# Moving small waits of TensorE in a two-layer transformer block: scale transposes behind products, a bias behind the next normalisation, expert transposes in another PSUM ring, ranks inside a gate pair

## The chip, the cores and the metric

The kernel runs on one core of one Trainium2 chip. The metric is the device time of one launch in microseconds (us); lower is better. All times below are microseconds unless marked ns.

## The reference

`x` is 8 x 256 rows of 512 numbers (2048 rows in all), `ctx` is a context of the same shape. Four residual steps follow each other:

```python
x = x + L0_xattn(ctx, ctx, layernorm(x), ssm_kernel, D, 8)   # long convolution of k*v pairs along 512, times q
x = x + L0_ffn(layernorm(x), w1, b1, w2, b2)                  # two "bit" linears, 512 -> 2048 -> 512
x = x + L1_xattn(layernorm(x), ctx, ...)                      # 16 heads of 32, 256 queries x 256 image keys per batch
x = x + L1_ffn(layernorm(x), ...)                             # 2 shared experts + top 2 of 16 routed experts

def _bitlinear(x, w, b):
    xq = round(layernorm(x) * 127 / max|.|) ...               # per row, 8 bits
    wq = clip(round(w / mean|w|), -1, 1) * mean|w|            # ternary weights
    return einsum('bsd,fd->bsf', xq, wq) + b
# L0_ffn: bitlinear(gelu(bitlinear(x, w1, b1)), w2, b2)
# L1_xattn: softmax(rms_norm(x@Wq+bq)*gq . rms_norm(ctx@Wk_img+bk)*gk / sqrt(32)) @ v, then @ Wo + bo
# L1_ffn: x + shared + sum over the two best experts of p_e * expert_e(x),
#         expert(x) = (gelu(x@g + gb) * (x@w1 + b1)) @ w2 + b2
```

## The kernel before

The 2048 rows live in SBUF as 16 tiles of 128 x 512 (`xs`). Five stages follow each other, and inside each stage the order of instructions on every engine is the order of the Python code (`in_order`); a scheduler does not move them. Each engine works its own queue strictly in turn, so an instruction that waits holds everything behind it on its engine.

**Stage 1, long convolution** (to about 185 us): a loop over 32 heads (`head`, called with `between`, which slips in small pieces of the next stage: `second_norm`, `mixed`, and `ahead`, the generators `Pair.gradually` that normalise and quantise the first two pairs of row tiles piece by piece).

**Stage 2, the bit FFN** (about 185 to 380): a software pipeline over eight pairs of tiles, `f0` to `f7` (class `Pair`). For a pair, `split` (GpSimd/POOL) cuts a per-row scale `u` into three bf16 parts; `turn_x` transposes the quantised rows on TensorE (PE) into `xT`, which ScalarE (ACT) copies to `xq`; `turn_u` transposes the scale parts into `uT`, which ACT copies to `ub` (L384). `hidden(i, half)` makes 8 products `xq` by `w1q` (L399), 2 bias products `ub` by `b1k` (L404), and a GELU on ACT (L408). `mean`, `centre` (L422), `squares` (L430, ACT), `largest` (L435, DVE), `scales`, `scales_back`, `rounded_back` (L453, VectorE/DVE) quantise the hidden rows; `turn_back` transposes them (`hT`, PE) and ACT copies them to `hq`; `back` makes 16 products (L473). In step `g` of the loop, pair `g` is in `hidden`, pair `g-1` is being quantised, pair `g-2` is in `turn_back` and `back(0)`, pair `g-3` in `back(1)`, and pair `g+1` is being normalised. PSUM rings: `tr` (two buffers) for all transposes, `conv` (two) for the hidden products, `mm` (two) for `op`.

**Stage 3, attention** (about 380 to 749): 64 steps; a step holds four heads' half, steps go in twos. In loop turn `n`: `normalise` of step n-1 (POOL, `pr`, L1244), exponentials of an odd step (ACT, L1235), scores of two steps (PE, `sc`), `turn` of step n-2 (8 transposes `pt`, L1255, ring `tr`), pieces of the next batch (`middle`, `value`, `end`: `k_mm`, `q_mm`, `v_mm`, their transposes), `values` (`o`, ring `mm`), and each fourth turn `project_out` (`fo`, ring `mm`), whose result DVE adds to `xs` (L1287) and to which POOL adds the output bias `bo` (L1288). In the last turns (`at` = n-56) there is no further batch; ACT normalises finished tiles for the experts (`dxn`, L1374), and `turn_in` transposes them (`dxT`, ring `tr`) and DVE copies them to `xT` (L1314).

**Stage 4, shared experts on half the rows and routing** (about 749 to 847): `gate` makes 4 fp32 products for one gate or up projection (`gu`, L1504), `gated` the GELU and product. The generator `route` (`pieces`) is drawn out between them: it computes on DVE which experts each row takes (`both`, L1573), counts ranks by 17 small products on PE (`rank`, L1577 on), derives the slots on DVE, and scatters the rows to DRAM by 32 indirect DMAs from POOL (L1633).

**Stage 5, routed experts** (about 847 to 1061): `Unit` (256 rows) and `Double` (2 x 64 rows). A unit loads weights and its gathered rows `xr` (SP queue), `turn` transposes them (`r_xTp`, L162, ring `gh`) and ACT copies them to `r_xT` (L1676), `products` (L1689) and `back` (L1705) follow. Then the shared experts on the other half of the rows, gathering, and the store.

Of the kernel before, what the change touches and what calls it, by code (L numbers as in the profile page):

```python
# [11 lines left out]
AF = mybir.ActivationFunctionType  # L12
ALU = mybir.AluOpType
# [6 lines left out]
DC = D // P  # L20
NT = B * S
H, HD = 32, 8
# [3 lines left out]
FF = 2048  # L26
# [52 lines left out]
def tile_kernel(ctx: ExitStack, tc: tile.TileContext, a: dict, out: bass.AP):  # L79
    nc = tc.nc  # L80
# [17 lines left out]
    zero = column(0.0, "zero")  # L98
# [59 lines left out]
    def transposed(pool, src, name, tag, chunks=range(DC)):  # L158

        ps = pool.tile([P, DC, P], F32, tag=tag, name=name)  # L160
        for at, c in enumerate(chunks):
            nc.tensor.transpose(ps[:, at, :], src[:, c * P : (c + 1) * P], ident)  # L162
# [123 lines left out]
    class Pair:  # L286
# [32 lines left out]
        def gradually(self):  # L319

            nm = self.nm
            self.mv = stat.tile([P, 2, 2], F32, tag="mv", name=nm + "_mv")
            for i in range(2):
                moment(self.mv[:, i, :], self.T[i], f"{nm}{i}")
                yield
            nmean = stat.tile([P, 2], F32, tag="nmr", bufs=2, name=nm + "_nm")
            times(nmean, self.mv[:, :, 0], -1.0)
            self.factor()
            yield
            self.xc = fp.tile([P, 2, D], F32, tag="xc", bufs=2, name=nm + "_xc")  # L330
            for i in range(2):
                nc.scalar.activation(
                    self.xc[:, i, :], self.T[i], AF.Identity, bias=nmean[:, i : i + 1]
                )
            yield
            self.largest_x()
            yield
            qs = self.scales_x()
            for i in range(2):
                nc.scalar.activation(  # L340
                    self.xc[:, i, :], self.xc[:, i, :], AF.Identity, bias=qmagic,
                    scale=qs[:, i : i + 1],
                )
            yield
            self.split()

        def largest_x(self):
            self.amax = stat.tile([P, 2], F32, tag="amax", name=self.nm + "_amax")
# [43 lines left out]
        def hidden(self, i, half):  # L392

            hp = pp.tile([P, FF // 2], F32, tag="conv", name=f"{self.nm}_hp{i}{half}")
            for q in range(2):
                cols = bass.ts(2 * half + q, D)
                dst = hp[:, q * D : (q + 1) * D]
                for c in range(DC):
                    nc.tensor.matmul(  # L399
                        dst, lhsT=self.xq[:, i, c, :], rhs=w1q[:, c, cols], start=(c == 0), stop=False  # L400
                    )
            for q in range(2):
                cols = bass.ts(2 * half + q, D)
                nc.tensor.matmul(  # L404
                    hp[:, q * D : (q + 1) * D], lhsT=self.ub[:, i, :], rhs=b1k[:, cols],
                    start=False, stop=True,
                )
            nc.scalar.activation(  # L408
                self.hs[i][:, bass.ts(half, FF // 2)], hp, AF.Gelu, bias=zero,
                scale=self.s1[:, i : i + 1], accum_out=self.hsum[:, i, half : half + 1],  # L410
            )

# [43 lines left out]
            self.hq = [None, None]  # L456

        def turn_back(self, i, half):
            if half == 0:
                self.hq[i] = fp.tile([P, FC, P], BF16, tag="hq", bufs=2, name=f"{self.nm}_hq{i}")  # L460
            ps = turned_halves(
                pp, [self.hs[i][:, bass.ts(2 * half + k, D)] for k in range(2)], f"{self.nm}_hT{i}{half}"
            )
            nc.scalar.activation(
                self.hq[i][:, bass.ts(half, 2 * DC), :], ps.rearrange("p i c q -> p (i c) q"),
                AF.Identity, bias=nhalf,
            )

# [283 lines left out]
    def between():  # L752
        if unfinished:
            sums(*unfinished)
        if 1 <= h <= 13:
            next(norm1)
        elif 17 <= h <= 24:
            next(mixed0)
        elif h > 24:
            next(ahead[0], None)  # L760
        for _ in range((0, 1, 3)[max(h - H + 3, 0)]):
            next(ahead[1])

    for g in range(H // G):
        kv, qx = following
        for hh in range(G):
            h = g * G + hh
# [227 lines left out]
    def more_mixed():  # L995
        for _ in range(2):
            next(mixed1)

    one, two, three = pairs[:3]
    one.turn_x()  # L1000
    one.turn_u()
    one.hidden(0, 0)
    for _ in ahead[1]:
        pass
    more_mixed()
    one.hidden(0, 1)
    more_mixed()
    one.hidden(1, 0)
    more_mixed()
    one.hidden(1, 1)  # L1010
    more_mixed()

    mix.__exit__(None, None, None)
# [4 lines left out]
    wsb = {}  # L1018
# [34 lines left out]
    one.largest(1)  # L1053
    one.squares(1)
    one.scales()
    two.hidden(1, 1)
    one.scales_back()
    three.turn_x()
    two.mean()
    one.rounded_back()  # L1060
    for g in range(2, 8 + 2):
# [66 lines left out]
            continue  # L1128
        if left:
            left.back(1)  # L1130
        if p:
            p.turn_u()
        if mid:
            mid.centre()
            mid.largest(0)
        if left:
            left.update(1)
            left.add_bias()
        if mid:
            mid.squares(1)  # L1140
        if p:
            p.hidden(0, 0)
        last.turn_back(0, 0)
        if coming:
            coming.moments()
        if mid:
            mid.largest(1)
        prepare(0)
        if p:
            p.hidden(0, 1)  # L1150
        last.turn_back(0, 1)
        if coming:
# [40 lines left out]
    with tc.tile_pool(name="att", bufs=2) as ap_, tc.tile_pool(  # L1193
# [10 lines left out]
        class Step:  # L1204
# [60 lines left out]
            def values(self, before):  # L1265
# [11 lines left out]
                            )  # L1277
                nc.scalar.copy(self.oT[:, 2 * cp : 2 * cp + 2, :], op)

        def project_out(b, i, oT):  # L1280
# [7 lines left out]
            nc.gpsimd.tensor_tensor(T, T, wsb["bo"], ALU.add)  # L1288

        class Norm:  # L1290

# [18 lines left out]
        done_norms = {}  # L1310

        def turn_in(t, xn):
            ps = transposed(pc, xn, f"dxT{t}", "tr")
            nc.vector.tensor_copy(xTs[t // 4][:, :, t % 4 * P : (t % 4 + 1) * P], ps)  # L1314


# [9 lines left out]
        for n in range(len(steps) + 4):  # L1326
# [9 lines left out]
                    coming = batches[steps[n].b + 1]  # L1336
            if 0 < n <= len(steps):
                steps[n - 1].normalise()
            if coming:
                coming.begin(k)  # L1340
            if n < len(steps) and n % 2:
# [14 lines left out]
                    coming.value(k - 4)  # L1356
                coming.end(k)
            at = n - (len(steps) - 8)
            if at in (-3, -1):
                batches[-1].value((at + 3) // 2)  # L1360
            if at == 1:

                nmr = stat.tile([P, 8], F32, tag="nmr8", bufs=1, name="d_nmr")
# [28 lines left out]
                    project_out(s.b, s.i, s.oT)  # L1392
            if n in later:
                project_out(later[n].b, later[n].i, later[n].oT)

            for t in NORMED.get(at - 1, ()):
                turn_in(t, done_norms[t])
# [423 lines left out]
    order = [lambda e=e: Unit(f"r{e}", e, NS * P * e, NS * P) for e in range(E)]  # L1821
    for j in range(NO1 // 2):
        order.insert(4 * j + 3, lambda j=j: Double(j))
    units = [order[0]()]
    units[0].turn()
    for i in range(len(order)):
        if i + 1 < len(order):
            units.append(order[i + 1]())
        units[i].products()
        if i:  # L1830
            units[i - 1].turn_back()
        if i + 1 < len(order):
# [126 lines left out]
```

## Time and profile before

Three runs took 1156.17 us in the median (1151.67 to 1158.35).

| what | us |
|---|---|
| time of the profiled execution | 1151.6 |
| its span, first to last instruction | 1149.8 |
| PE busy | 1094.3 (95%) |
| DVE / ACT / POOL busy | 683.6 / 520.8 / 440.2 |
| mean granted TensorE clock | 0.999 |
| chain that ended last | PE 76%, DVE 14%, POOL 4% |

A row of a timeline has the start, the length, the engine and line, the operation, what it writes and reads, how many were merged, and in brackets how long its engine had idled before it and which instruction's end let it go. "PE pt L1255 <- DVE xT L1314" in the table of waits reads: PE stood before its instruction on `pt` until DVE's instruction on `xT` had ended. Busy PE is modelled from pipelined matmuls; the idle time between them is what this document argues with.

### The profile page before, as it was taken

How to read it: one execution, taken by the hardware profiler on the slowest of the kernel's cores; microseconds unless marked ns; L12 is line 12 of the kernel's file. 1: busy time of each engine (PE TensorE's matmuls, PEld its weight loads, DVE VectorE, ACT ScalarE, POOL GpSimd, SP SyncE). 2: the span in 40 equal slices, each digit the busy share in tenths (PEclk: the TensorE clock that was granted, in tenths of full speed). 3: DMA queues.
4: the chain of work that ended last, by engine and by line, in shares of the span. 5: the costliest groups of instructions: out<-in, count | busy, mean ns of one | idle time of the engine just before them, and what ended most of it. 6: DMA issues, size and time to landing. Idle time of an engine off the chain costs nothing.

```text
span 1149.8 us, 16488 instructions
## 1 busy us (share of the span) xinstructions
PE 1094.3 (95%) x5866; PEld 658.8 (57%) x5885; DVE 683.6 (59%) x1507; ACT 520.8 (45%) x1173; POOL 440.2 (38%) x501
## 2 busy tenths in 40 slices
PE   4999998899999999999999998899999999999997
PEld 3777775454545555555655555554466766675443
DVE  5998999798866565765656756637612222222452
ACT  4437645798884555656556565531011121111000
POOL 5788887244331243433333434313770000000650
PEclk9999999999999999999999999999999999999999
DMA  7424520699500100000000010052668999997571
GB/s 272 154 74 150 153 76 20 236 305 291 141 1 19 37 1 4 16 19 1 20 20 1 2 38 1 1 194 102 240 202 269 306 338 330 301 314 240 155 248 40
DMA packets 122780, 153.26 MB, mean 133 GB/s; under 512 B 7481, under 2 KB 81273, under 8 KB 122178
## 3 DMA queue, kind: packets, MB, share of 16 engines
q1 hardware_dynamic: 108608, 116.49, 32.1%
q10 hardware_dynamic: 8962, 18.85, 4.6%
q0 software_dynamic: 5120, 16.78, 4.4%
q8 instruction: 49, 0.80, 0.3%
q14 instruction: 41, 0.34, 0.1%
HBM read 107.66 MB, written 44.43 MB: 132 GB/s over the span
## 4 chain that ended last, share of the span: by engine, by line
PE 76%; DVE 14%; POOL 4%; issue 2%; ACT 1%; DMA 1%; SPq 1%; POOLq 0%; DVEq 0%; ACTq 0%
PE r_h L1689 10%; PE gu L1504 9%; PE y L693 5%; PE k_mm L865 5%; PE fo L1284 5%; PE v_mm L865 5%; PE r_po L1705 5%; PE q_mm L865 5%; PE po L1526 5%; PE pt L1255 5%; PE f_op L473 2%; PE sc L1219 2%; PE f_hp L399 2%; PE o L1274 2%; PE o_h L1746 2%
## 5 line engine op out<-in xcount | busy, mean ns | idle before, releaser
L1244 POOL TENSOR_TENSOR pr<-pr,rden 128x1024 f32<-128x1024 f32 x64 | 121.1, 1893 | 155.8 <-DVE rden L1242 140.6
L693 PE MATMUL y<-kv,tp 128*128 128x288 f32 x640 | 161.7, 408 | 5.2 <-DVE wl L716 5.0
L693 PEld LDWEIGHTS y<-kv,tp 128*128 128x128 f32 x640 | 119.0, 190 | 42.5 <-PE y L693 10.1
L1235 ACT ACTIVATE pr<-sc,mx 128x256 f32<-128x256 f32 x256 | 118.3, 483 | 8.1 <-DVE mx L1227 6.9
L1842 POOL DMA_INDIRECT yg<-yd,slot x32 | 33.1, 1035 | 224.4 <-PE gu L1504 206.3
L1689 PE MATMUL r_h<-r_xT,r_gu 128*128 128x256 f32 x512 | 113.7, 380 | 1.5 <-ACT r_xT L1676 1.5
L1689 PEld LDWEIGHTS r_h<-r_xT,r_gu 128*128 128x128 f32 x512 | 96.8, 190 | 22.4 <-issue 8.0
L1227 DVE TENSOR_REDUCE mx<-sc 128x4 f32<-128x1024 f32 x64 | 77.5, 1212 | 4.5 <-PE sc L1219 4.5
L1255 PE MATMUL pt<-ident,pr 128*128 128x128 f32 x512 | 70.6, 279 | 7.5 <-DVE xT L1314 3.5
L1696 DVE SCALAR_TENSOR_TENSOR r_y<-r_h,eb,r_ge 128x256 f32<-128x256 f32 x32 | 15.5, 483 | 97.7 <-PE r_h L1689 94.4
L1260 ACT COPY pts<-pt 128x512 f32<-128x512 f32 x64 | 37.8, 590 | 73.2 <-PE pt L1255 73.2
L1255 PEld LDWEIGHTS pt<-ident,pr 128*128 128x128 f32 x512 | 55.0, 140 | 26.1 <-issue 14.6
L1695 ACT ACTIVATE r_ge<-r_h,gb 128x256 f32<-128x256 f32 x32 | 15.1, 473 | 109.0 <-PE r_h L1689 109.0
L399 PE MATMUL f_hp<-w1q,f_xq 128*128 128x512 bf16 x245 | 59.4, 379 | 5.3 <-ACT f_xq L376 4.5
L631 POOL TENSOR_TENSOR kv<-kx 128x2048 f32<-128x2048 f32 x16 | 57.6, 3601 | 12.9 <-ACT kx L617 12.9
L865 PE MATMUL k_mm<-Wk_sb,cx 128*128 128x512 f32 x128 | 58.1, 598 | 0.0
L865 PE MATMUL v_mm<-Wv_sb,cx 128*128 128x512 f32 x128 | 57.7, 593 | 0.0
L1705 PE MATMUL r_po<-r_w,r_y 128*128 128x512 f32 x128 | 57.7, 593 | 0.0
L1284 PE MATMUL fo<-Wo_sb,oT 128*128 128x512 f32 x128 | 57.7, 593 | 0.0
L865 PE MATMUL q_mm<-Wq_sb,xT 128*128 128x512 f32 x128 | 57.6, 593 | 0.0
L1516 ACT ACTIVATE ge<-gu,gb 128x512 f32<-128x512 f32 x16 | 11.0, 687 | 102.6 <-PE gu L1504 93.8
L473 PE MATMUL f_op<-w2q,f_hq 128*128 128x512 bf16 x249 | 57.0, 379 | 0.4
(486 smaller groups left out, 2104.5 us busy)
## 6 DMA issues: line engine op xcount, KB each, us to landing
xd<-blank SPq DMA_DIRECT2D x1, 15360.0 KB, 59.2
tp<-kpd SPq DMA_DIRECT2D x32, 256.0 KB, 3.3
r_gu<-in_rg SPq DMA_DIRECT2D x16, 512.0 KB, 6.6
r_gu<-in_rw SPq DMA_DIRECT2D x16, 512.0 KB, 6.8
r_w<-in_rw SPq DMA_DIRECT2D x16, 512.0 KB, 6.8
r_xr<-xd SPq DMA_DIRECT2D x16, 512.0 KB, 6.9
yd<-r_yo ACTq DMA_DIRECT2D x32, 256.0 KB, 5.7
yd<-blank SPq DMA_DIRECT2D x1, 6144.0 KB, 77.9
```

What stands on the lines that cost most here:

```text
L399: nc.tensor.matmul(dst, lhsT=self.xq[:, i, c, :], rhs=w1q[:, c, cols], start=(c == 0), stop=False)
L473: nc.tensor.matmul(op, lhsT=self.hq[i][:, c, :], rhs=w2q[:, c, :], start=(c == 0), stop=(c == FC - 1))
L693: nc.tensor.matmul(y[:, ll, :, 0:PAIRS], lhsT=tp[:, dl : dl + P], rhs=view(kv, (m0 * G + hh) * PAIRS, [[G * PAIRS, B], [1, PAIRS]]), start ...
L865: nc.tensor.matmul(t, lhsT=lT[:, c, i * P : (i + 1) * P], rhs=w[:, c, :], start=(c == 0), stop=(c == DC - 1),)
L1227: nc.vector.tensor_reduce(self.mx, self.sc.rearrange("p r c k -> p (r c) k"), AX.X, ALU.max, negate=True)
L1235: nc.scalar.activation(self.pr[:, h // 2, h % 2, :], self.sc[:, h // 2, h % 2, :], AF.Exp, bias=self.mx[:, h : h + 1], accum_out=self.den[ ...
L1244: nc.gpsimd.tensor_tensor(flat, flat, rden.unsqueeze(2).to_broadcast([P, 4, S]), ALU.mult)
L1255: nc.tensor.transpose(pt[:, cc, k, :], self.pr[:, rr, cc, k * P : (k + 1) * P], ident)
L1284: nc.tensor.matmul(fo, lhsT=oT[:, c, :], rhs=wsb["Wo"][:, c, :], start=(c == 0), stop=(c == DC - 1))
L1504: nc.tensor.matmul(ps, lhsT=w[0][:, c, k, f * P : (f + 1) * P], rhs=xTs[tb][:, c, :], start=(c == 0), stop=(c == DC - 1),)
L1689: nc.tensor.matmul(ps, lhsT=self.w[0][:, c, k, f * P : (f + 1) * P], rhs=self.xT[:, c, 0:n], start=(c == 0), stop=(c == DC - 1),)
L1705: nc.tensor.matmul(po, lhsT=self.y[:, f, i * P : (i + 1) * P], rhs=self.w[1][:, f, :], start=(f == 0), stop=(f == EC - 1),)
```

## The change

Every instruction stays; only places in the queues and one PSUM ring change.

1. *FFN start.* `split` moves ahead of the last `yield` of `gradually`, so that it is drawn one head earlier. Of the second pair's pieces one less is drawn in the last head; that piece (ACT, centring of `f1_xc`) comes after `turn_u` of the first pair. The first pair's first two `hidden` follow each other; the four pairs of `mix` transposes come later, the last four tiles in a row.
2. *FFN, pair f2.* `turn_u` comes before the loop, and ACT makes `xq` and `ub` of f2 ahead of f1's last GELU. In step 2 both halves of `hidden(0)` come ahead of the first `hT`.
3. *FFN, steps 3 to 7.* The two `uT` transposes, and the eight transposes of the first `hT`, move from either side of the first `hidden` to between its 8 products and its 2 bias products. ACT's order stays: `ub`, `squares`, GELU, `hq`.
4. *Attention.* POOL's bias add goes behind the `normalise` of the following turn. `turn_in` takes ring `mm` in place of `tr`. The last batch's first `value` moves from turn 53 to 52.
5. *Routing.* The rank products go between the gate and the up projection of one pair, not ahead of both; the DVE, ACT and POOL orders do not change by it.
6. *Routed experts.* The second unit's transposes move ahead of the first unit's products. On SP only one load of `o0_xr` changes places with one of `r3_gu`.

```diff
@@ Pair.gradually
+            self.split()
             yield
-            self.split()
@@ Pair.hidden is now product + gelu
+        def hidden(self, i, half, between=None):
+            self.product(i, half, between)
+            self.gelu(i, half)
 ...                                    # 8 products
+            if between:
+                between()
 ...                                    # 2 bias products
@@ Pair.turn_back is now turn (PE) + turned (ACT)
@@ between, in the heads
-        for _ in range((0, 1, 3)[max(h - H + 3, 0)]):
+        for _ in range((0, 1, 2)[max(h - H + 3, 0)]):
@@ FFN start
     one.turn_u()
+    next(ahead[1])
     one.hidden(0, 0)
+    one.hidden(0, 1)
+    more_mixed()
     for _ in ahead[1]:
         pass
-    more_mixed()
-    one.hidden(0, 1)
-    more_mixed()
     one.hidden(1, 0)
     more_mixed()
     one.hidden(1, 1)
+    more_mixed()
     more_mixed()
@@
-    two.hidden(1, 1)
+    two.product(1, 1)
     one.scales_back()
     three.turn_x()
+    three.turn_u()
+    two.gelu(1, 1)
     two.mean()
@@ loop over g
-        if p:
-            p.turn_u()
 ...
-        if mid:
+        def turns():
+            if g > 2:
+                p.turn_u()
             mid.squares(1)
+            if g > 2:
+                last.turn(0, 0)
         if p:
-            p.hidden(0, 0)
-        last.turn_back(0, 0)
+            p.hidden(0, 0, turns)
+        if g == 2:
+            p.hidden(0, 1)
+        if g == 2 or not p:
+            last.turn(0, 0)
+        last.turned(0, 0)
@@ attention
-            nc.gpsimd.tensor_tensor(T, T, wsb["bo"], ALU.add)
+            biased.append(T)          # added by add_output_bias(), called behind normalise()
-            ps = transposed(pc, xn, f"dxT{t}", "tr")
+            ps = transposed(pc, xn, f"dxT{t}", "mm")
-            if at in (-3, -1):
-                batches[-1].value((at + 3) // 2)
+            if at in (-4, -1):
+                batches[-1].value((at + 4) // 3)
@@ shared experts and routing
-    for (tb, e, f), n in zip(rest, (2, 3, 3, 3, 3, 2)):
-        gated(tb, e, f, gate_up(tb, e, f, shw[e]), yTs[tb])
+    for (tb, e, f), n in zip(rest, (0, 2, 3, 3, 3, 3)):
+        first_gate = gate(tb, e, f, shw[e], 0)
         for _ in range(n):
             next(pieces)
+        gated(tb, e, f, (first_gate, gate(tb, e, f, shw[e], 1)), yTs[tb])
+    for _ in range(2):
+        next(pieces)
@@ routed experts
-    units = [order[0]()]
-    units[0].turn()
+    units = []
+    for i in range(2):
+        units.append(order[i]())
+        units[i].turn()
     for i in range(len(order)):
-        if i + 1 < len(order):
+        if 0 < i < len(order) - 1:
             units.append(order[i + 1]())
```

More of the change, by code (lines that the diff above doesn't have):

```diff
@@ L390, in turn_u, with product @@
             self.hsum = stat.tile([P, 2, 2], F32, tag="hsum", name=nm + "_hsum")
-        def hidden(self, i, half):
+        def hidden(self, i, half, between=None):
+            self.product(i, half, between)
+            self.gelu(i, half)
+        def product(self, i, half, between=None):
             hp = pp.tile([P, FF // 2], F32, tag="conv", name=f"{self.nm}_hp{i}{half}")
+            self.hp = hp
             for q in range(2):
@@ L407, in hidden, with gelu @@
                 )
+        def gelu(self, i, half):
             nc.scalar.activation(
-                self.hs[i][:, bass.ts(half, FF // 2)], hp, AF.Gelu, bias=zero,
+                self.hs[i][:, bass.ts(half, FF // 2)], self.hp, AF.Gelu, bias=zero,
                 scale=self.s1[:, i : i + 1], accum_out=self.hsum[:, i, half : half + 1],
@@ L458, in turn_back, with turn, turned @@
         def turn_back(self, i, half):
+            self.turn(i, half)
+            self.turned(i, half)
+        def turn(self, i, half):
             if half == 0:
                 self.hq[i] = fp.tile([P, FC, P], BF16, tag="hq", bufs=2, name=f"{self.nm}_hq{i}")
-            ps = turned_halves(
+            self.ps = turned_halves(
                 pp, [self.hs[i][:, bass.ts(2 * half + k, D)] for k in range(2)], f"{self.nm}_hT{i}{half}"
             )
+        def turned(self, i, half):
             nc.scalar.activation(
-                self.hq[i][:, bass.ts(half, 2 * DC), :], ps.rearrange("p i c q -> p (i c) q"),
+                self.hq[i][:, bass.ts(half, 2 * DC), :], self.ps.rearrange("p i c q -> p (i c) q"),
                 AF.Identity, bias=nhalf,
@@ L1148, in tile_kernel @@
         prepare(0)
-        if p:
+        if p and g > 2:
             p.hidden(0, 1)
@@ L1278, in values @@
                 nc.scalar.copy(self.oT[:, 2 * cp : 2 * cp + 2, :], op)
+        biased = []
         def project_out(b, i, oT):
@@ L1287, in project_out, with add_output_bias @@
             nc.vector.tensor_tensor(T, T, fo, ALU.add)
-            nc.gpsimd.tensor_tensor(T, T, wsb["bo"], ALU.add)
+            biased.append(T)
+        def add_output_bias():
+            while biased:
+                T = biased.pop()
+                nc.gpsimd.tensor_tensor(T, T, wsb["bo"], ALU.add)
         class Norm:
@@ L1338, in tile_kernel @@
                 steps[n - 1].normalise()
+            add_output_bias()
             if coming:
@@ L1394, in tile_kernel @@
                 project_out(later[n].b, later[n].i, later[n].oT)
+            if n == len(steps) + 3:
+                add_output_bias()
             for t in NORMED.get(at - 1, ()):
@@ L1831, in tile_kernel @@
             units[i - 1].turn_back()
-        if i + 1 < len(order):
+        if 0 < i < len(order) - 1:
             units[i + 1].turn()
```

## The prediction, made before the changed kernel ran

> **What bounds the kernel now.** I read the busy times first, then the chain that ended last, then PE's waits by releaser, then windows by stage, and last the timeline around each wait.
>
> ```profile
> PE 1094.3 (95%) x5866; PEld 658.8 (57%) x5885; DVE 683.6 (59%) x1507; ACT 520.8 (45%) x1173; POOL 440.2 (38%) x501
> PE 76%; DVE 14%; POOL 4%; issue 2%; ACT 1%; DMA 1%; SPq 1%; POOLq 0%; DVEq 0%; ACTq 0%
> ```
>
> TensorE is busy for 1094.3 of 1149.8 us, so all its idle time is 55.5 us. No instruction is removed; the change can only win parts of those 55.5 us, where PE waits for something that is late. PE's waits by releaser (total, count, mean) show which of them it aims at:
>
> ```profile
> PE f_uT L382 <- POOL u L366: 4.5, 4, 1.4
> PE f_hp L399 <- ACT f_xq L376: 4.5, 3, 2.2
> PE pt L1255 <- DVE xT L1314: 3.5, 5, 1.9
> PE pt L1255 <- POOL pr L1244: 3.2, 3, 2.0
> PE rank L1577 <- DVE both L1573: 1.8, 1, 1.8
> PE f_hp L404 <- ACT f_ub L384: 1.8, 1, 1.8
> PE r_h L1689 <- ACT r_xT L1676: 1.5, 2, 0.7
> PE qT_tr L162 <- DVE pts L1262: 1.3, 1, 1.3
> ```
>
> These are 22.1 us in all: the most that could be won here if every one vanished and none came back. The windows say where another engine would take over (length, then busy PE, PEld, DVE, ACT, POOL, the clock, DMA share, GB/s):
>
> ```profile
> 245.00:338.00 93.00, 89.95 (x559) 47.41 (x571) 77.23 (x141) 80.84 (x94) 39.73 (x89) 1.00 0.63 176
> 682.00:749.00 67.00, 57.68 (x553) 36.18 (x552) 42.19 (x83) 38.77 (x130) 29.49 (x18) 1.00 0.01 1
> ```
>
> In the FFN's steady part ACT (87%) and DVE (83%) stand close behind PE (97%), so a wait won there can come back. In the attention's tail nothing but PE is above 63%: there, waits are matters of order, and can be moved.
>
> **FFN start (edit 1): 2.1 us.** Before, `uT` waited 1.35 for `split`, which POOL did at 193.20 to 194.97, and the first product waited 1.55 for `xq`, which stood on ACT behind `f1_xc` (194.63, 1.33 long). Drawn one head earlier, `split`'s nine instructions (1.8 us) find `f_u` ready at 188.16 and POOL idle from 187.05 to 190.82: they hide there; without that cover they would delay the next head's combination by up to 1.8. `uT` follows `xT` at once, `xq` runs at 193.73 to 194.83, and the first product starts at 194.85 instead of 197.02: 2.17 earlier. The four `mix` groups now come last, where two buffers and DVE's adds (0.64 each) make PE wait about 0.85 in place of 0.38 + 0.34. `f1_xc`, moved behind `xq` and `ub`, ends at 196.5; its own transposes come about 208, and cover it. Bounds: 1.5 to 2.5. I take 2.1.
>
> **Pair f2 and steps 3 to 7 (edits 2 and 3): 2.9 us.** These rows of before carry it:
>
> ```profile
> 224.35 1.90 PE L399 MATMUL f_hp<-w1q,f_xq 128*128 128x512 bf16 x8 [2.18 <-ACT f_xq L376]
> 225.75 2.00 ACT L418 ACTIVATE f_h<-f_h,f_hm 128x2048 f32<-128x2048 f32 x1 [1.45 <-DVE f_hm L115]
> 242.59 2.47 DVE L453 TENSOR_SCALAR f_h<-f_h,f1hq_qs 128x2048 f32<-128x2048 f32 x2
> 242.72 1.19 POOL L365 CAST f_up<-f_u 128x2 bf16<-128x2 f32 x1
> 245.17 0.44 PE L382 MATMUL f_uT<-ident,u 128*128 128x128 f32 x2 [0.88 <-POOL u L366]
> ```
>
> At 224.35 PE waited 2.18 for `xq`, which stood behind a GELU (1.20); now it stands ahead, so about 1.0 goes. The 1.81 for `ub`, queued behind `mean` (225.75, which itself waits for DVE's `f_hm`), goes whole, since `ub` comes ahead too. But that does not shorten `mean`: the GELU of f2's first half still follows `mean` (to 227.65), `squares` (2.00) and itself (1.19), to 230.95, and the third `hidden` needs its `conv` buffer. So PE, now early, waits about 2.35 there, and starts it at 230.95 where it started at 231.56: of 2.8 won, 0.6 is left, and the two `hT` wait for no one. In steps 3 to 7, `uT` waited 0.88, 1.18 and 1.12 (3.18 in all) for `u`; between the products it comes 1.73 after them (L399 to L404: 245.44 to 247.17), with the 16 products before it ending at 244.29 at about 245.9, and `u` is ready at 245.11. What is late next is `ub`, 2.20 after the first product, and behind it on ACT `squares` (2.00) and the GELU (1.19): with 0.27 for `ub` the buffer is free at 5.66 after it, and PE wants it at 5.47 (16 products 3.46, 4 of bias 0.86, `uT` 0.27, two groups of `hT` 0.88): 0.15 to 0.2 a step, 0.75 in five. The stretch's waits were (with f1's `xq`, 0.77, and one for a GELU, 0.24) 0.77 + 0.24 + 2.18 + 1.81 + 3.18 = 8.2, and becomes 0.77 + 0.24 + 1.18 + 2.35 + 0.75 = 5.3. Bounds: zero, if ACT and DVE take the loop whole, to 5.4, if the 2.35 and 0.15 don't appear.
>
> [...]
>
> **Attention's tail (edit 4): 4.7 us.**
>
> ```profile
> 708.80 1.26 POOL L1288 TENSOR_TENSOR xs<-xs,bo_sb 128x512 f32<-128x512 f32 x1 [3.82 <-DVE rden L1242]
> 710.03 3.75 POOL L1244 TENSOR_TENSOR pr<-pr,rden 128x1024 f32<-128x1024 f32 x2
> 711.98 1.09 PE L1255 MATMUL pt<-ident,pr 128*128 128x128 f32 x8 [2.03 <-POOL pr L1244]
> 731.48 0.39 ACT L1278 COPY oT<-o 128x256 f32<-128x256 f32 x1
> 732.82 0.66 PE L1255 MATMUL pt<-ident,pr 128*128 128x128 f32 x4 [1.89 <-DVE xT L1314]
> ```
>
> At 708.80 the bias takes POOL for 1.26 ahead of `pr` that PE waits 2.03 for; `rden` was there at 708.81. Behind it, `pr` starts 1.23 earlier: 1.23. The bias then runs 1.89 later; it is read by the moments of finished tiles, which come much later, and by `dxn`. Around 686 to 692 three waits (0.87, 1.28, 0.17) would be covered by `v_mm`, moved there (8 products, 3.44), but `oT`'s copy then stands on ACT for `o`, the exponentials behind it end at 691.2, and the scores come at about 692.3 instead of 693.6: 1.3. With `dxT` in ring `mm`, the transposes `pt` no longer need DVE's copy of `xT` to free a `tr` buffer: waits of 0.35, 0.35, 1.89, 0.51 and 0.44 go. At the 1.89 the next `fo` finds `oT` only at 731.87, so 1.4 of it counts; and in `mm` new small waits come, for `oT` or `xT`'s copy ahead of `fo` (0.3 at 722, 0.4 at the end): 2.2 net. Sum 1.3 + 1.2 + 2.2 = 4.7. Bounds: 2 (half of each goes into the next wait) to 6.5.
>
> **Ranks (edit 5): 1.8 us.** The ranks waited 1.83 at 783.67 for `both`; 8 products of the gate (3.44) now stand ahead, so the wait is covered whole. The chain behind begins about 1.4 later, but DVE idles 1.62 at 791.91, and the scatter comes no later. Bounds: 1 to 1.83.
>
> **Experts (edit 6): 1.5 us.** Two waits of 0.73 (848.33 and 857.10) for ACT's copy of `xT` are each covered by the other unit's transposes (1.04). But the second unit's rows are needed 9 us earlier:
>
> ```profile
> 837.07 0.89 SPq L1668 DMA_DIRECT2D r_xr<-xd  x2
> 846.57 1.04 PE L162 MATMUL r_xTp<-ident,r_xr 128*128 128x128 f32 x8
> 848.33 7.17 PE L1689 MATMUL r_h<-r_xT,r_gu 128*128 128x256 f32 x32 [0.73 <-ACT r_xT L1676]
> ```
>
> Both loads are issued at 837.07 behind the last scatter and land by 842.4; PE comes by at 846.57 - 1.83 + 1.04 = 845.8, 3.4 later. The swap of `o0_xr` and `r3_gu` on SP is much later, of loads that PE needs still later: nothing. Bounds: 0.7 to 1.5.
>
> **Sum.** 2.1 + 2.9 + 4.7 + 1.8 + 1.5 = 13.0. The profiled execution took 1151.6 (span 1149.8), so a profile after should show a span near 1136.8. That execution is 4.6 below the median of the three runs, 1156.17, whose fastest is 1151.67; from the median the time is 1156.2 - 13.0 = 1143. By the bounds the gain is 5.2 (1.5 + 0 + 2 + 1 + 0.7) to 17.8 (2.5 + 5.4 + 6.5 + 1.8 + 1.5).
>
> **Rivals.** *The waits only move on.* ACT and DVE set the FFN (87% and 83%), so its start and steps give nothing, and the tail half: 2.3 + 1.7 + 1.5 = 5.5, 1150.7. For it: of f2's 2.8 I already lose 2.2 so. Against it: DVE's loop, from one rounding to the next, went down to 17.75 (262.23 to 279.98), while PE's step without a wait is 18.05 to 18.16. 0.12.
>
> *`u` is late again.* If in four steps a third cast falls into the centring (L422, at 244.98 for 1.27), `u` is ready at 246.25 and not at 245.11, 0.35 after its new place: 1.4 less, 1144.6. Against it: root, scalars and casts start from one DVE instruction, and so keep their distance. 0.10.
>
> *ACT's gaps absorb the new waits.* The 2.35, the 0.75 and some 1.0 of the tail don't appear: 17, 1139. 0.12.
>
> *The gather decides, and it gets slower.* A late landing of the second unit's rows now holds the first unit's products too, us for us, from 845.8 on (before, from 855.34). To lose it must eat 13.0 and 5.8 more: landing near 865, 28 us from the issue where these loads take 6.9 in the median, 8.5 at most (846.0 with 0.45 for the second issue: 0.2 lost). The time would be 1163. 0.04.
>
> That the change would not move what it says is excluded by the two programs' order: counts are equal, and the places are those named.
>
> **How the numbers follow.** A measurement of this kernel can tell about 0.5%, 5.8 us. The forecast, 1143, has 0.62; it, the late `u` and the absorbed waits are all below 1150.4: 0.84 faster. The waits that only move on are within 0.5%: 0.12. Slower: 0.04. The range goes from 1135 (a gain above the high bound, with the runs' own spread of some us) to 1151 (the first rival).
>
> **What would show it.** Right: `uT` idles nowhere in the FFN, `xq` starts near 193.7, the third `hidden` of step 2 idles some 2.3 on `f_h`; no `pt` row is released by `xT`; `rank` and the first `r_h` follow without a gap; the span is near 1136.8. Wrong: a new row of waits over 3 us on L404 or L399 by L408 (first rival), POOL casts of 1.2 ahead of `uT` (second), or `r_xTp` idling on a DMA (fourth).

## The result, and the profile after

The changed kernel took 1143.02 us in the median (four runs, 1142.12 to 1143.72), the kernel before 1155.01 (1151.67 to 1158.35): a ratio of 0.9905, 95% interval 0.9878 to 0.9932. The forecast was 1143, faster. The number was right. Its working was not quite: the profiled execution became 7.9 us shorter (span 1149.8 to 1141.9), not 13.0, and the rest of the median's 12 us came from somewhere the prediction did not look. Most of what follows is about that.

The page of the changed kernel, busy times and chain:

```profile
PE 1099.7 (96%) x5885; PEld 662.1 (58%) x5885; DVE 686.2 (60%) x1507; ACT 519.6 (46%) x1173; POOL 443.0 (39%) x501
PE 75%; DVE 18%; ACT 2%; POOL 2%; issue 2%; DMA 0%; ACTq 0%; POOLq 0%; DVEq 0%
```

PE is busy 5.4 us longer. The instructions are the same; 19 more of them are on record, and part of it is that. The other part is that some matmuls became slower, as the windows show. PE's waits (total, count, longest; in the prediction's list, too, the third number is the longest and not the mean), those that answer to the eight shown before:

```profile
PE f_hp L404 <- ACT f_h L417: 2.9, 2, 2.6
PE f_hp L404 <- ACT f_xq L376: 2.6, 3, 1.0
PE pt L1281 <- POOL pr L1270: 1.4, 2, 1.0
PE fo L1312 <- ACT oT L1304: 1.1, 1, 1.1
PE f_hT L171 <- DVE f_h L462: 0.6, 1, 0.6
```

The rows for `uT`, `ub`, `pt` by `xT`, `rank` and `r_h` are gone. The largest new one, 2.6 before a `hidden` of f2 for a GELU, was forecast (2.35). The last, 0.6 for DVE's rounded rows, was not. The places of the ranks and of the first units in the timeline:

```profile
781.08 0.28 PE L1614 MATMUL rank<-both,ones 128*128 128x272 bf16 x1
840.53 1.91 PE L162 MATMUL r_xTp<-ident,r_xr 128*128 128x128 f32 x16
842.30 14.08 PE L1726 MATMUL r_h<-r_xT,r_gu 128*128 128x256 f32 x64
```

No bracket stands behind these rows: PE does not idle before the ranks, nor before either unit's products. The second unit's rows landed at 838.25 and were needed at 841.41.

The windows around two places (length, then busy PE, PEld, DVE, ACT, POOL, the clock, DMA share, GB/s) show why PE's busy time grew:

```profile
226.30:229.70 3.40, 0.77 (x9) 0.45 (x7) 3.37 (x3) 3.40 (x5) 0.00 (x0) 1.00 1.15 348
229.70:233.10 3.40, 3.40 (x9) 1.21 (x8) 3.30 (x7) 2.76 (x4) 1.21 (x4) 0.50 1.15 348
711.00:714.40 3.40, 2.12 (x18) 1.42 (x20) 1.94 (x5) 3.40 (x16) 2.37 (x2) 1.00 0.00 0
714.40:717.80 3.40, 3.40 (x20) 2.34 (x16) 1.92 (x3) 0.88 (x2) 1.89 (x1) 0.50 0.02 5
```

Twice the granted clock falls to 0.50, each time for 3.41 us (229.70 to 233.11 and 714.39 to 717.80 in the trace's clock record), each time behind a stretch in which PE did little: 0.77 of 3.40 us in the one; 2.12 of 3.40 in the other, in transposes and products on 32 rows, with a wait. The profiled execution of before has no such window between its first 18 us and its last three. Eight products that took 1.90 us take 3.23:

```profile
229.31 3.23 PE L404 MATMUL f_hp<-w1q,f_xq 128*128 128x512 bf16 x8 [2.63 <-ACT f_h L417]
```

The starts of the same matmul in both traces give the ledger: how much earlier each stands in the changed kernel.

| place | before | changed | earlier by |
|---|---|---|---|
| first product of the FFN | 197.02 | 194.83 | 2.19 |
| f1's `xT` | 210.23 | 208.42 | 1.81 |
| third `hidden` of f2 | 231.56 | 229.31 | 2.25 |
| first of 16 `f_op`, behind the half-clock window | 234.16 | 233.60 | 0.56 |
| eleventh `f_op` | 327.96 | 325.14 | 2.82 |
| first scores of the attention | 380.53 | 378.38 | 2.15 |
| fifth `fo` from the end | 678.82 | 677.59 | 1.23 |
| scores near 690 | 693.61 | 691.12 | 2.49 |
| first `lgT` (routing) | 749.56 | 745.53 | 4.03 |
| first `r_xTp` | 846.57 | 840.53 | 6.03 |
| first `r_po` | 864.99 | 857.09 | 7.90 |

### The profile page after: what moved, and what is told of

Its sections match the earlier page's. It is cut to its first block, busy times and chain, and to the rows that moved or that the text cites. A ratio compares the mean times of both kernels' runs of the same rounds, so it can differ in the third digit from the quotient of the medians.

```text
span 1141.9 us, 16502 instructions
## 1 busy us (share of the span) xinstructions
PE 1099.7 (96%) x5885; PEld 662.1 (58%) x5885; DVE 686.2 (60%) x1507; ACT 519.6 (46%) x1173; POOL 443.0 (39%) x501
## 4 chain that ended last, share of the span: by engine, by line
PE 75%; DVE 18%; ACT 2%; POOL 2%; issue 2%; DMA 0%; ACTq 0%; POOLq 0%; DVEq 0%
PE r_h L1726 10%; PE gu L1541 10%; PE y L708 5%; PE v_mm L880 5%; PE r_po L1742 5%; PE q_mm L880 5%; PE po L1563 5%; PE f_op L488 4%; PE pt L1281 4%; PE k_mm L880 3%; PE f_hp L404 3%; PE fo L1312 3%; DVE mx L1253 2%; PE sc L1245 2%; PE o L1300 2%
## 5 line engine op out<-in xcount | busy, mean ns | idle before, releaser
L404 PE MATMUL f_hp<-w1q,f_xq 128*128 128x512 bf16 x256 | 61.8, 386 | 5.5 <-ACT f_h L417 2.9
```

The source lines that it names most:

```text
L404: nc.tensor.matmul(dst, lhsT=self.xq[:, i, c, :], rhs=w1q[:, c, cols], start=(c == 0), stop=False)
```

## The experiments

Times are medians. "Clock" is the mean granted clock of a run. The theory tested first: the waits that went explain the profile, and the clock explains the medians.

**The kernel before, as a control.** No edit.

> The kernel before, unchanged, as a control. The changed kernel's profile is 7.9 us shorter than that of before, its median 12 us shorter: the kernel before spreads over 6.7 us (1151.67 to 1158.35), the changed one over 1.6. Theory A, the clock: in before's slow executions the granted clock falls to one half in windows of 3.41 us, as at 229.70 and 714.39 of the changed kernel; then its runs show a mean clock below 0.999, lower by 0.0015 for each window and longer by up to 1.7 us each, four windows for 6.7 us. Theory B, not the clock: the clock stays at 0.998 to 0.999 in all runs and the time differs by some us nevertheless, because of transfers or of the instructions' loading; then the profile shows where against 1149.8.

Measured: 1155.69 (10 runs, 1151.36 to 1158.58), ratio 1.0002 (0.9983 to 1.0021). The runs fall into groups by their clock: 1151.4 and 1151.9 at 0.999; 1155.1 to 1156.8 at 0.995 or 0.996; 1158.4 to 1158.6 at 0.991. All 44 runs of the kernel before whose clock was noted do the same: 12 at 0.998 or 0.999 (1151.3 to 1152.6), 23 at 0.995 or 0.996 (1154.7 to 1157.1), 9 at 0.991 (1158.0 to 1158.6). Theory A holds, as far as time goes with clock: no execution of the two slower groups was profiled. The profile from which the prediction was worked out had 0.999, like the 12; the median is one of the 23, some 4 us above.

**FFN as before.** Edits 1, 2 and 3 taken back in the changed kernel:

```diff
-            self.split()
             yield
+            self.split()
 ...                       # hidden and mix in turn; turn_u, squares and hT around hidden, as before
```

> The changed kernel with the FFN's edits (1, 2 and 3) undone. Two questions. The waits: by the prediction 5.0 us are lost (2.1 start, 2.9 steps), to 1147; by the ledger of the two profiles (first product 2.19 earlier, end of the FFN only 2.15 earlier) 2.2 to 2.5, to 1144.5. The clock: the kernel before shows mean clocks of 0.999, 0.995 and 0.991, 1151.4, 1156 and 1158.4 us. Theory A, one of the two places where it loses its clock is the FFN: this kernel then shows 0.995 in about half of its runs, about 4 us longer. Theory B, both are elsewhere: its clock stays at 0.997 or above in all runs.

Measured: 1145.05 (1143.88 to 1146.09), clock 0.997 to 0.999 in all five runs; 2.0 us slower than the changed kernel. In its profile the FFN ends 2.95 later than in the changed one (381.33 against 378.38), with one half-clock window at 196.35 that cost 0.8; the changed one had a window that cost 1.69. Without either the FFN's edits are worth 2.95 - 0.8 + 1.69 = 3.8; in the medians 2.0, near the 2.2 to 2.5 of the ledger, with a clock that is lower in the changed kernel (0.995 to 0.998). 5.0 is neither. And the FFN is not where the kernel before loses 4 us: Theory B.

**Attention as before.** Edit 4 taken back:

```diff
-            biased.append(T)
+            nc.gpsimd.tensor_tensor(T, T, wsb["bo"], ALU.add)
-            ps = transposed(pc, xn, f"dxT{t}", "mm")
+            ps = transposed(pc, xn, f"dxT{t}", "tr")
-            if at in (-4, -1):
-                batches[-1].value((at + 4) // 3)
+            if at in (-3, -1):
+                batches[-1].value((at + 3) // 2)
```

> The changed kernel with the attention's edit (4) undone: bias, ring and value as before. The waits: 4.4 us are lost in the tail and 0.9 won back in the steady part, 3.5: 1145.7. The clock, theory A: the attention's tail, where between 682 and 745 only transposes and products on 32 rows or columns stand between the large products, is a place where the kernel before loses its clock; then runs with 0.995 or less and some 4 us more appear here. Theory B: the tail is not; clock 0.997 or above in all runs.

Measured: 1148.71 (10 runs, 1145.20 to 1150.32), 5.7 slower than the changed kernel. Only two runs stand at 0.998 (1145.2 and 1145.6, as the waits alone would have it); the other eight are at 0.994 or 0.992. The windows of its profile show where:

```profile
711.20:714.60 3.40, 3.40 (x37) 2.69 (x30) 2.06 (x5) 3.40 (x15) 0.48 (x2) 0.50 0.00 0
731.70:735.10 3.40, 3.40 (x6) 1.32 (x5) 1.33 (x5) 1.56 (x4) 1.10 (x1) 0.50 0.02 5
```

One window stands behind the wait of 2.03 for `pr`, the other behind the 1.89 for `xT`. The attention's tail, with its old waits, is the place where the clock goes: Theory A. The edit is worth about 3 us of waits and in the median another 3 of clock. In this one profile the two windows cost only 1.7 together (72.47 from the fifth `fo` from the end to the routing, 70.74 in the kernel before): from the transposes that waited 2.03 to the next `fo` it takes 10.73, in the kernel before 10.72, so the waits that follow took the first window up.

**The bias alone, at its old place.**

```diff
-            biased.append(T)
+            nc.gpsimd.tensor_tensor(T, T, wsb["bo"], ALU.add)
```

> The changed kernel with the output bias added at its old place, directly behind DVE's addition. Theory A, the bias in the steady part costs: there it runs 0.18 later beside DVE's c_t, which waits for it, five times; with the old place the stretch from 378 to 677 is 0.9 us shorter than in the changed kernel. The tail then is longer: the wait for pr at 708 comes back, 1.0 (measured gain 1.04), and near 686 v_mm covers the rest, 0 to 0.3. Sum: 0.1 to 0.4 us slower than the changed kernel, no difference that a time can show; the parts show in the profile. Theory B, the bias behind the normalisation is what won near 690 too: then 1.3 more is lost there, and the kernel is 1.4 us slower than the changed one.

Measured: 1142.05 (1141.23 to 1144.19; clock 0.995 to 0.999). From the first scores to 678 it gains nothing and loses 0.05, where the changed kernel loses 0.92. The wait for `pr` is 2.03 again, and near 690 nothing is lost (1.26 won, as in the changed kernel, so it is not the bias that won there): Theory A. What the late bias costs in the steady part is seen in DVE's `c_t`, an instruction on two columns. Before, it stands beside POOL's `pr`:

```profile
470.15 1.89 POOL L1244 TENSOR_TENSOR pr<-pr,rden 128x1024 f32<-128x1024 f32 x1
471.69 0.37 DVE L139 TENSOR_TENSOR c_t<-c_r 128x2 f32<-128x2 f32 x1
```

In the changed kernel `pr` comes first, and the bias stands beside it:

```profile
468.82 1.26 POOL L1322 TENSOR_TENSOR xs<-xs,bo_sb 128x512 f32<-128x512 f32 x1
469.55 0.55 DVE L139 TENSOR_TENSOR c_t<-c_r 128x2 f32<-128x2 f32 x1
```

A like `d_t` takes 0.15. Both times `c_t` ends with POOL's instruction (472.06 and 472.04; 470.10 and 470.08), and the changed order lets that end 0.18 later against DVE; `k_pre` behind it, and PE's `k_mm`, are later by as much, in five batches 0.9. All five `c_t` end 0.02 behind POOL's instruction, in both profiles; why was not tried.

**The bias late in the tail only.**

```diff
-            biased.append(T)
+            if n >= 51:
+                biased.append(T)
+            else:
+                nc.gpsimd.tensor_tensor(T, T, wsb["bo"], ALU.add)
 ...                       # project_out is given the turn, n
```

> The changed kernel with the bias behind the normalisation only from turn 51 on, and at its old place before that. Theory A: the steady part gains the five waits of 0.18 back, the tail keeps what it won: 0.9 us faster than the changed kernel, 1142.1. Theory B, the late c_t is a matter of chance, not of the bias: no change in the stretch 378 to 677, 1143.

Measured: 1141.36 (1141.10 to 1142.52), ratio to the kernel before 0.9874 (0.9842 to 0.9907). The steady stretch loses 0.01 against before, where the changed kernel loses 0.92. Theory A.

**f2's first GELU ahead of f1's mean.**

```diff
     two.gelu(1, 1)
+    three.product(0, 0)
+    three.gelu(0, 0)
     two.mean()
 ...                       # and step 2 of the loop leaves hidden(0, 0) out
```

> The changed kernel with the GELU of f2's first half ahead of f1's mean on ACT, so that the third hidden of step 2 need not wait 2.63 for it. Theory A, the wait is a matter of order: the 2.63 vanish, and with them the window of half clock behind it (1.7 where it falls): 2 to 4 us faster than the changed kernel. Theory B, ACT is full here: the transposes of the next half then wait for ACT's hq copies instead (mean, squares and a GELU still stand ahead of them, to about 231 to 232), and the first back starts at about 232.1 instead of 233.6: 1.5 us where a half-clock window had fallen there, 0.3 where not.

Measured: 1140.60 (1140.20 to 1142.06). The wait of 2.63 is gone, and this one stands in its place:

```profile
231.68 1.01 PE L171 MATMUL f_hT<-ident,f_h 128*128 128x128 f16 x8 [2.38 <-ACT f_hq L479]
```

Theory B: the order moved the wait to the next thing that ACT owes PE, and the first `back` starts 37.20 after the first product in place of 38.77. The clock's window fell behind it too (231.63), in the profiled run. In three of the four runs the clock was 0.998 to 1.000 and the time 1140.2 to 1140.7, so the order helps a little; by how much beyond the clock, these runs don't tell.

**Steps 3 to 7 as before**, f2 and the start changed.

```diff
+        if p and g > 2:
+            p.turn_u()
 ...
-            p.hidden(0, 0, turns)
+            p.hidden(0, 0)
 ...                       # squares ahead of it, turn_back behind it
```

> The changed kernel with edit 3 undone for steps 3 to 7 (uT ahead of the products, hT behind the bias products); edit 2 for f2 stays. Theory A, the prediction's: the waits of 0.88, 1.18 and 1.12 for u come back and 2.4 is lost against the changed kernel at the FFN's end. Theory B, DVE's and ACT's chain sets these steps: u's waits come back in the profile, but PE finds the transposes hT and the conv buffers ready later anyway, and the FFN's end moves by at most 0.6.

Measured: 1143.06 (1142.83 to 1143.30; clock 0.997 to 0.999). `u`'s waits are back:

```profile
PE f_uT L382 <- POOL u L366: 2.8, 3, 1.1
```

and the attention starts 1.40 later than in the changed kernel (379.78 against 378.38), 1.26 counted from the FFN's first product. That is neither 2.4 nor 0.6: about half of the 2.8 is won by the edit. Both profiles have a half-clock window near 229.6. The medians (1143.06 against 1143.02) don't show it: the clocks of the two sets of runs differ (0.997 to 0.999 here, 0.995 to 0.998 there).

**The ring alone.** `dxT` in `tr` again.

> The changed kernel with dxT in ring tr again; bias and value stay changed. The waits: pt waits for xT's copy as before, and of the 2.1 that the two profiles show between 717 and the routing 1.5 to 2.1 is lost. The clock: with edit 4 undone as a whole, 8 of 10 runs showed 0.994 or 0.992, with windows of half clock at 711 and 732. Theory A, the ring's waits are what lets the clock fall there (transposes and waits alone between two projections): runs at 0.994 or less appear again. Theory B, it is the bias ahead of pr (the wait of 2.03): the clock stays at 0.995 or above here.

Measured: 1146.00 (1144.72 to 1146.71; clock 0.997 to 0.999). From the `fo` near 702 to the routing it wins 1.04 on the kernel before; the next experiment, undisturbed there and with the ring changed, wins 3.17: the ring is worth 2.1. PE's waits:

```profile
PE pt L1281 <- DVE xT L1348: 3.7, 4, 2.4
```

The clock stays above 0.995: Theory B as to the ring, but the bias alone did not bring the low clocks back either. Either it takes more than one of the old waits together, or it is the place of `value`, which was not taken back alone; these runs (four of each) don't say which. This profile has a further wait that the change does not explain (1.5 for DVE's `xs` in the routing, 828.9); see the last section.

**Ranks and second unit as before.** Edits 5 and 6 taken back.

```diff
-        first_gate = gate(tb, e, f, shw[e], 0)
 ...
+        gated(tb, e, f, gate_up(tb, e, f, shw[e]), yTs[tb])
 ...
-    for i in range(2):
-        units.append(order[i]())
-        units[i].turn()
+    units = [order[0]()]
+    units[0].turn()
```

> The changed kernel with edits 5 (ranks) and 6 (second unit's transposes) undone. The prediction's waits: 1.83 and twice 0.73, 3.3 lost, in the routing and in the first two units. The two profiles show 2.0 and 1.87 won, 3.9. Either way 1146 to 1147; the windows around the ranks (781 to 785) and the first units (838 to 858) show which, and no place else moves.

Measured: 1145.83 (1144.94 to 1146.19). The waits are back as they were:

```profile
PE rank L1614 <- DVE both L1610: 1.8, 1, 1.8
PE r_h L1726 <- ACT r_xT L1713: 1.5, 2, 0.7
```

From the first `lgT` to the first `r_po` it wins 0.00 on the kernel before, where the changed kernel wins 3.87 (4.03 to 7.90): 2.0 up to the first `r_xTp`, which holds the ranks, and 1.87 at the units. (The two edits were taken back together; the places in the timeline tell them apart.) No half-clock window fell between 20 and 1139 us in this profile. So it is the clean look at the stages ahead: FFN from its first product to the attention 1.61 won, where the changed kernel's profile with its window shows 0.04 lost (the window cost 1.65, and nothing took it back); attention's tail 4.42 won.

**f2 as before.** Edit 2 taken back.

```diff
-    two.product(1, 1)
+    two.hidden(1, 1)
     one.scales_back()
     three.turn_x()
-    three.turn_u()
-    two.gelu(1, 1)
     two.mean()
 ...                       # and step 2 of the loop as before
```

> The changed kernel with edit 2 undone (f2's scale transposes, GELU order and step 2 as before), steps 3 to 7 changed. Theory A, the prediction's: 0.5 to 0.6 of the third hidden of step 2 is lost, and stays lost at the FFN's end. Theory B: nothing is lost, since the wait of 2.63 and the half-clock window behind it, which this order lacks (its waits are 2.2 and 1.8 with products between them), cost the changed order more: this kernel is equal or up to 1.5 us faster.

Measured: 1146.14 (1143.22 to 1147.55). Its profile has no half-clock window in the FFN, and from the first product to the attention it wins 1.19, against 1.61 in the last experiment: edit 2 is worth 0.4 there, Theory A. But that holds without a window only. Of the seven profiles that have the wait of 2.63, six have a half-clock window behind it. The five of these in which nothing else of the FFN differs lose 0.05 to win 0.14 from the first product to the attention. Beside them the old order of f2, with its 1.19, is 1.1 to 1.2 shorter, as Theory B said: in most profiled executions edit 2 costs more clock than it wins in waits. The median cannot show it: 2.95 of waiting for DVE's `xs` and a half-clock window (828.65) fell into the routing, which the edit doesn't touch.

**Both improvements together**: the bias late from turn 51, and f2's GELU first.

> The changed kernel with the bias behind the normalisation only from turn 51 on, and f2's first GELU ahead of f1's mean. If both gains add: 0.9 us of the steady part and 0.2 to 1.5 of the FFN, 1140 against 1142.5. If the FFN's steps take back what f2 wins: 1141.3, as with the bias alone.

Measured: 1140.40 (1139.23 to 1141.55), ratio to the kernel before 0.9890 (0.9857 to 0.9923). Two runs at clock 0.999 took 1139.2 and 1139.6, two at 0.997 took 1141.2 and 1141.6. In the profile the steady part has its 0.9 back, and the FFN, with a window at 231.65, is 0.2 shorter than in the changed kernel. Every run is faster than each of the changed kernel's four (1142.12 to 1143.72), but the two ratios to the kernel before, 0.9890 and 0.9905, have intervals that overlap, and from f2's GELU alone (1140.60) the runs don't tell it apart.

**Squares later still**, on top of the last one.

```diff
         last.turn_back(0, 1)
+        if g == 2:
+            mid.squares(1)
 ...                       # and no longer ahead of hidden in step 2
```

> The kernel with the bias late only from turn 51 on and f2's first GELU ahead of f1's mean, and f1's second squares behind the two hq copies of step 2 on ACT. There hT of the third half waited 2.38 for hq (ACT full). Theory A, it was the squares' place: the wait falls to 0.3 and the first back starts 2 us earlier, 1138.5 against 1140.4. Theory B, DVE's chain through steps 2 and 3 sets the pace: the back starts earlier, and later PE waits for f1's rounded rows or f3's by the same 2 us; 1140.

Measured: 1141.71 (1140.80 to 1142.97). The first `back` starts at 229.92, and the wait for `hq` is 0.26, but then

```profile
237.76 0.80 PE L171 MATMUL f_xT<-ident,f_xc 128*128 128x128 f16 x8 [1.61 <-DVE f_xc L315]
```

PE waits for DVE's rounded rows of f3. From the first product to the attention it wins 1.77, the clean look 1.61: of the 2.4 won at `back` (2.42 against 0.03, counted from the first product), 0.2 is left. Theory B. Here DVE's chain sets the FFN's pace.

## Why the prediction was right, and where only its number was

By the prediction's own steps; the clock's two windows (1.69 at 229.7, from 2.25 earlier to 0.56; 1.62 at 714.4, from the fifth `fo` from the end to the routing 67.94 against 66.32 in the clean look) are counted by themselves:

| step | predicted | measured | by |
|---|---|---|---|
| FFN start | 2.1 | 1.8 | ledger, f1's `xT` |
| f2 | 0.5 | 0.4 | ledger; edit 2 taken back 0.4 |
| steps 3 to 7 and after | 2.4 | 1.6 | ledger; edit 3 taken back 1.3 |
| steady attention | 0 | -0.9 | ledger; bias taken back |
| attention's tail | 4.7 | 4.4 | clean look; ledger 2.8 + 1.6 of window |
| ranks | 1.8 | 2.0 | edits 5 and 6 taken back |
| experts | 1.5 | 1.9 | the same |
| sum | 13.0 | 11.2 | |
| clock windows | 0 | -3.3 | windows |
| profile | 13.0 | 7.9 | spans |

**Right.** The mechanisms of the start (first product 2.19 earlier, 2.17 said), of f2's new wait (2.63 in place of the 1.81 and half of the 2.18, 2.35 said), of the tail (1.26 near 690, 1.3 said; 1.04 for `pr`, 1.2 said; 2.1 for the ring, 2.2 said), of the ranks and of the experts were as described, down to the landing of the second unit's rows 3.2 ahead of need (3.4 said). Of the signs named beforehand the span missed (1141.9, not 1136.8), and casts of 1.19 and 1.14 ahead of `uT`, the second rival's sign, stand in four steps (before in three). Most casts take 0.18 or 0.19; these end 0.04 or 0.05 behind one of DVE's two `rounded_back` (243.91 and 245.11 against 243.87 and 245.06 before). None starts beside the centring, so that one would be held there as well was my estimate, not shown; and `u` is ready in time, no `uT` waits. Two sums were off without moving the forecast: the FFN's high bound would be 6.0 with the 0.15 taken off in all five steps, not 5.4, and the upper bounds as given add up to 17.7; the fourth rival's time would be 1162.

**Mis-sized: the steps.** `u`'s waits went: 3.18 of idle time, 3.8 from start to start (before, a step takes 17.99 or 18.00 from its first product to that of the next where `u` is ready, 19.39 and 19.32 where not, and the first of the three waits came to 1.10). But each step pays more than the 0.15 to 0.2 that I gave the `conv` buffer: in the clean look the bias products start 0.63 after `hT`, where back-to-back it is 0.45 (they wait for `ub`, 0.18, which I had taken as ready), and the third `hidden` 0.57 instead of 0.45 (0.12): 0.3 a step, and every step takes 18.31. Then, in step 8, `hT` waits 0.6 for DVE's rounding, and 0.7 is lost: PE had come too early for DVE. So 3.8 - 5 x 0.3 - 0.7 = 1.6 in place of 2.4. The rival "waits only move on" is right in part here, as the last experiment shows most plainly.

**Missed: the steady part.** I priced the late bias only in the tail, where PE waited for it. It is moved in every batch, and in five it pushes DVE's `c_t`: 0.9.

**Missed: the clock.** The prediction set the profiled 1151.6 beside the median 1156.17 and took the 4.6 between them as spread, and subtracted 13.0 from the median. The 4.6 had a cause that the change touches: half-clock windows, which by the experiments fall mostly in the attention's tail, behind its waits (inferred from the kernel with the attention as before, since no execution of the kernel before at 0.996 or less was profiled). With these waits shortened, the changed kernel's runs go from 0.995 to 0.998 where those of before go from 0.991 to 0.999. So the median's 12.0 are the profiles' 7.9 (11.2 of waits less 3.3 of windows), 3.4 by which the median of before stands above its profiled execution (1155.01 against 1151.6), and 0.7 by which the changed kernel's stands below (1143.02 against 1143.72); 1143 was not hit with 13 of waits. That the two errors cancelled is luck; the sign and the size of the largest steps are not. One step of the change brought a window with it: the new wait of 2.35 of f2 was priced at its length, and in six of seven profiles it drew half clock behind it.

The changes of the granted clock stand on a grid. Both half-clock windows of the changed kernel's profile are 3.413 long in the trace's clock record; from the start of the one (229.70) to that of the other (714.39) are 142.0 such lengths, and the stretches at full clock before, between and behind them (211.63, 481.28 and 419.84) are 62.0, 141.0 and 123.0. Ahead of 229.70 PE was busy for 0.77 of 3.40 us, ahead of 714.40 for 2.12, with transposes and products on 32 rows. That half clock follows such work as it follows idle time is a reading of these rows and not shown by an experiment.

The grid is also my reading of why a kernel loses its clock in some executions only. Of the 4586 windows of such grids in all fourteen profiles (without the start and the end), the eleven in which PE was busy for less than 1.4 of 3.41 us (0.78 to 1.38) all have half clock behind them; of the 34 with 1.4 to 2.2 two have it (1.53 and 2.13); of the others none. Where the grid falls differs from one execution to the next: its first edge on record is 17.58 in the profile of before, 18.07 in the changed kernel's. In the changed kernel the wait of 2.63 lies in one window (226.29 to 229.70, 0.78 busy); in the clean look the grid cuts the same wait in two (2.37 and 1.83 busy), and the clock stays. Slid along the profile of before, such a window finds less than 1.4 at five places, when it starts near 194 or 222 in the FFN or near 685, 709 or 730 in the tail; along the clean look at one, f2's wait. At 0.0015 of mean clock each, five would make about the 0.991 of the slowest runs; that is an estimate from these profiles.

## What to carry to other kernels

Look up the clock of every run before setting a profiled execution beside a median: where runs fall into groups by clock, the profile shows one group, and a stretch of some 3 us in which PE does little (0.77 of 3.40 at f2) costs its wait and, in some of the profiled runs, up to 1.7 us of half clock behind it. Such a stretch can also be made by the change itself, as f2's shows. When a wait is taken out of a pipeline that two other engines nearly fill, ask at each of them what it owes next; f2's wait moved from GELU to `hq` to DVE's rounding, and 0.2 of 2.4 was won. An instruction moved in a loop must be priced at every turn, against the engine beside whose instructions it then runs, not only where its old place hurt.

## What the runs showed of the hardware that was not expected

The granted clock of one core falls to 0.50 for 3.41 us at a time, in the same kernel in some executions and not in others; the kernel before takes 1151.3 to 1152.6, 1154.7 to 1157.1 or 1158.0 to 1158.6 by it. A DVE instruction on two columns (`c_t`, 0.15 alone) takes 0.55 in five batches, and ends 0.02 behind the POOL instruction beside it; `f_hm` in the FFN, as small and 0.16 to 0.19 alone, takes 1.27 where POOL's addition of `b2b` (1.26) starts just ahead of it (261.04 and 298.42 before, 241.39 in the changed kernel). And in three profiles (ring, f2 and squares) PE stood 1.5 to 2.95 in the routing near 825 for DVE's `xs`, with POOL's scatters stopping for 3 to 5 us, in instructions that stand as in the changed kernel, whose profile has none of it; POOL's stop of 3.1 appears also with edits 5 and 6 taken back, without cost to PE. All four are profiles of one set of runs on one chip; in the ten others, of other sets, a scatter follows the last within 1.75 us. So it goes with that set or chip rather than with an edit; what makes the scatters late was not tried and stays open, and the four medians of that set can hold some of it.
